# Gathering one tile at a time and evicting turned shares two PSUM banks at a time, in a dynamic-filter convolution followed by a bottleneck block

## The chip, the cores and the metric

The kernel runs on one core of a Trainium2 chip. The engines named below are PE (TensorE, matrix products and transposes), ACT (ScalarE), DVE (VectorE), POOL (GpSimd) and SP (SyncE, which issues most of the DMAs). PE writes into PSUM, eight banks of 512 fp32 columns on 128 partitions; the other engines copy from there into SBUF. Times are microseconds on the device, of one execution of the whole program. Where a time is read inside the program it counts from the start of the profiled span.

## The reference

Everything is fp32. The first layer takes x of 4 x 256 x 64 x 64 and computes, for every pixel, 49 weights from x itself; these then weigh 49 shifted copies of x:

```python
k = conv(x, w1, rhs_dilation=2, padding=6) + b1      # 7x7, 256 -> 128 channels
k = conv(k, w2) + b2                                 # 1x1, 128 -> 49
attn = softmax(k, axis=1)                            # over the 49 taps
y = einsum('bkchw,bkhw->bchw', shifts, attn)         # shifts[k] = x moved by 2*(u-3), 2*(v-3)
```

The second layer is a bottleneck block on y: 1x1 convolution (256 to 64), batch normalisation and ReLU, 3x3 convolution, batch normalisation and ReLU, 1x1 convolution (64 to 256), batch normalisation, plus y, ReLU. The normalisations use the moments of the data.

## The kernel before, in words

The two convolutions of the first layer are folded into one with 49 output channels, and this one is computed from sums of columns of x at several points, so that fewer products are needed. The input lies in one large SBUF buffer, the arena: four planes of 8192 columns each, xs[h][c]. Up to about 411 us PE runs the products of L361 over "pieces" of this buffer, while DVE makes their operands (L321 to L324 in make, L337 in add_columns) and combines the results (L371, L398, L389 on ACT). Final products (L437) turn the combined sums, called sides, into logits, and final_add puts them into place with DVE additions (L371).

The logits are handled in eight groups (s, h), s = 0 to 3 and h = 0 or 1. For each group five steps follow.

- exponents: DVE takes the maximum over the 49 taps (L479) and subtracts it (L480); ACT takes the exponential (L481).
- totals: DVE sums (L488) and takes the reciprocal (L489).
- shares: DVE multiplies and writes the four parts j = 0 to 3 into a row of zeroed, padded columns (L502). For the group (3,1), POOL clears a few places again (L513).
- turns: for each j, eight PE transposes (L522) fill two PSUM banks with the turned shares; two ACT copies (L529) bring them into the matrix amat, one for each half g of the columns. In the last group, (3,1), the copy of g = 1 is DVE's (L527).
- zero_edges: after both groups of an s, POOL clears ten strips of amat (L537).

amat takes the place of x in the arena, columns 0 to 32767, when the planes of x are no longer needed in that place. Its order is (g, x, c, m, e): g has a stride of 16384 columns, x (the group and j % 2) 1024, c (j // 2) 512. Some other things lie in the same columns while amat is being filled: planes of x that later pieces still read, the sides of the last chunk (from column 8192), and two of the padded rows (11264 to 15935 and 28096 to 32767).

All this is written in an order fixed by hand (manual_schedule, from L571). Inside the convolution, single steps are put between its groups of products by the table fill (L541 to L567): the turns (0,0) stand in one chunk, the turns (0,1) and (1,0) in a later one, and the first two turns of (1,1) in the last. After the convolution come the rest of the turns (1,1), the last final products, and then the sequence of L730 to L751. Engines other than the writer are released by semaphores, which the framework places from what each instruction reads and writes.

Then the gather computes y. A unit is one of the batch's images b and one quarter q of its pixels; 16 units are taken in the order of `units`. For a unit, more_xt loads the rows of x in pixel-major form by three DMAs (load_xt, L142, L143, L148), and shift_xt makes a second tile, shifted by 64 rows, with one ACT copy (L152, partitions 0 to 63) and two POOL copies (L153, L154). For each unit and each half of the channels, gather (L823) makes 32 products (64 records in the trace): for c = 0 from the tile itself and for c = 1 from the shifted one, 7 inner block pairs and one pair of edge blocks for each, by two halves of the output partitions. keep_y (L847) evicts the two banks, by DVE (L858) or, for the second half of the channels, by ACT (L856), and stores y by a DMA (L859). The convolution to 64 channels (conv1, L862) follows for every pair of units, and more_xt is called for the units that come. Two units' tiles exist at a time. From L777 a second part in hand-written order covers the first call of more_xt; the order of what follows it comes from the framework.

The last stages are the 3x3 convolution, the moments for the third normalisation, and the 1x1 convolution to 256 channels with the output.

Of the kernel before, what the change touches and what calls it, by code (L numbers as in the profile page):

```python
# [42 lines left out]
F32 = mybir.dt.float32  # L43
AF = mybir.ActivationFunctionType
ALU = mybir.AluOpType
AX = mybir.AxisListType
PSUM = bass.MemoryType.PSUM

P = 128
# [51 lines left out]
def conv_seq_kernel(ctx: ExitStack, tc: tile.TileContext, xp, xt, w1, b1, w2t, b2, m1t, g1, be1,  # L101
                    m2t, g2, be2, m3t, g3, be3, z, mask, pavg, out, ydram):
    nc = tc.nc

    def pool(stack, name, bufs, space=None, **kw):
        if space is not None:
            kw["space"] = space
        return stack.enter_context(tc.tile_pool(name=name, bufs=bufs, **kw))
# [14 lines left out]
    smp = pool(ctx, "smp", 3)  # L123
# [9 lines left out]
    amat = arena[:, :AT].rearrange("p (g x c m e) -> p g x c m e", g=2, x=R // 2, c=2, e=4)  # L133
    XT = NT * C
    xts = {}
# [203 lines left out]
    def bank(cn, k):  # L339
        return accall[:, (6 * cn + k) % 8]  # L340
# [130 lines left out]
    def columns(s, h):  # L471

        return logit[:, 2 * s + h].rearrange("p j (w k) -> p j w k", k=K)

    def exponents(s, h):

        e = columns(s, h)
        mx = smp.tile([P, 4, 4], F32, tag="mx", name="mx")
        nc.vector.tensor_reduce(mx, e, AX.X, ALU.max)  # L479
        nc.vector.tensor_tensor(e, e, mx.unsqueeze(3).to_broadcast([P, 4, 4, K]), ALU.subtract)  # L480
        nc.scalar.activation(e, e, AF.Exp)  # L481

# [2 lines left out]
    def totals(s, h):  # L485

        sm = smp.tile([P, 4, 4], F32, tag="sm", name="sm")
        nc.vector.tensor_reduce(sm, columns(s, h), AX.X, ALU.add)  # L488
        nc.vector.reciprocal(sm, sm)  # L489
        factors[s, h] = sm  # L490
# [3 lines left out]
    def shares(s, h):  # L494

        e = columns(s, h)
        sm = factors.pop((s, h))
        row = pads[ROWS[s, h]]
        for j in range(4):
            o = 32 + 32 * (j % 2)  # L500
            taps = row[j][:, :, o : o + 32 * K7].rearrange("p w (u x) -> p w u x", x=32)[:, :, :, :K7]
            nc.vector.tensor_tensor(  # L502
                taps,
                e[:, j].rearrange("p w (u v) -> p w u v", v=K7),
                sm[:, j].unsqueeze(2).unsqueeze(3).to_broadcast([P, 4, K7, K7]),
                ALU.mult,
            )

            for w in range(3):
                if s == 0 and h == 0:  # L510
                    nc.gpsimd.memset(taps[:, w, :, : 3 - w], 0.0)
                if s == NS - 1 and h == 1:
                    nc.gpsimd.memset(taps[:, 3 - w, :, 4 + w :], 0.0)  # L513

    def turn(s, h, j, b0, shared=False):

        row = pads[ROWS[s, h]]
        pt = accall[:, b0 : b0 + 2].rearrange("p a (m n) -> p (a m) n", n=P)
        for k in range(2):
            for w in range(4):  # L520
                o = 35 - (WS * s + 4 * h + w) + P * k
                nc.tensor.transpose(pt[:, 4 * k + w, :], row[j][:, w, o : o + P], ident)  # L522
        for g in range(2):
            dst = amat[:, g, 2 * (2 * s + h) + j % 2, j // 2].rearrange("p (n k) e -> p k n e", k=2)
            src = pt[:, :, 64 * g : 64 * g + 64].rearrange("p (k w) n -> p k n w", k=2)
            if shared and g:
                nc.vector.tensor_copy(dst, src)  # L527
            else:
                nc.scalar.copy(dst, src)  # L529

    def zero_edges(s):

        for g in range(2):
            for c, above, below in ((0, ((0, 96),), ((96, P),)), (1, ((0, 32),), ((32, 64), (64, P)))):
                for block, parts in ((0, above), (2 * NT - 1, below)):
                    for p0, p1 in parts:
                        nc.gpsimd.memset(amat[p0:p1, g, 4 * s : 4 * s + 4, c, block :: 2 * NT, :], 0.0)  # L537
# [8 lines left out]

    second, third, between, final = ("pair", 1, 1), ("pair", 2, 1), ("last", LAST, 1), ("pair", NP - 1, 1)
    put(second, 0, 5, lambda b0: exponents(0, 0))
    put(second, 1, 1, lambda b0: (totals(0, 0), shares(0, 0)))
    put(third, 1, 2, lambda b0: exponents(0, 1))  # L550
    put(third, 2, 0, lambda b0: totals(0, 1))
    put(third, 2, 3, lambda b0: exponents(1, 0))
    put(third, 3, 0, lambda b0: totals(1, 0))
    put(between, 0, 1, lambda b0: shares(0, 1))
    for j in range(4):
        put(second, 2, j, lambda b0, j=j: turn(0, 0, j, b0))
        put(between, 0 if j < 3 else 1, (j + 3) % 6, lambda b0, j=j: turn(0, 1, j, b0))
        put(between if j < 3 else final, 1 if j < 3 else 0, j + 3 if j < 3 else 2, lambda b0, j=j: turn(1, 0, j, b0))
# [12 lines left out]
    with tc.manual_schedule(engines=engines):  # L571
# [66 lines left out]
        for q, (cn, h, sub, step, count) in enumerate(pieces):  # L638
            kind, n, c = chunks[cn]
# [19 lines left out]
            elif waiting and step:  # L659
                total, slots = len(waiting), 6 * (count - 1 - step) + 2  # L660
                for i in range(total):
                    s = (2 * i + 1) * slots // (2 * total)
# [25 lines left out]
            if kind == "early":  # L688
# [6 lines left out]
                pt = bank(cn, 6)[:, :K]  # L695
# [3 lines left out]
            elif step == count - 1 or (chunks[cn][0] == "pair" and cn != end and step == 1):  # L699
                k = uses.index((cn, h)) + 2  # L700
# [24 lines left out]
        def turns(s, h, js, shared=False):  # L725
            for j in js:
                turn(s, h, j, (6 * end + 2 + 2 * n_turn[0]) % 8, shared)
                n_turn[0] += 1
# [7 lines left out]
        turns(2, 0, (0, 1))  # L736
        run_adds()
        nc.gpsimd.memset(pads_flat[3], 0.0)
        exponents(3, 0)
        turns(2, 0, (2, 3))  # L740
        totals(2, 1)
        shares(2, 1)
        exponents(3, 1)
        turns(2, 1, range(4))
        zero_edges(2)
        for h in range(2):
            totals(3, h)
            shares(3, h)
        turns(3, 0, range(4))
        turns(3, 1, range(4), True)  # L750
        zero_edges(3)  # L751
# [71 lines left out]
    def gather(n, half):  # L823

        b, q = units[n]
        m = (b // 2 * Q + q) * 2 * NT
        pts = [bank(0) for c in range(2)]
        for edge in (False, True):
            for c in range(2):
                x = xts[b, q, c]  # L830
                for i in (0,) if edge else range(1, NT):

                    o = 64 * (i - 1)
                    blocks = slice(m, m + 2 * NT, 2 * NT - 1) if edge else slice(m + 2 * i - 1, m + 2 * i + 1)
                    dst = pts[c].rearrange("p (m n) -> p m n", n=64)
                    for part in HALVES:
                        nc.tensor.matmul(  # L837
                            dst[part, :: NT - 1] if edge else pts[c][part, o : o + 128],
                            x[:, i, half * P + part.start : half * P + part.stop],
                            amat[:, b % 2, :, c, blocks, :].rearrange("p x m e -> p m x e"),  # L840
                            start=(i == 1),
                            stop=edge,
                            skip_group_check=True,
                        )
        return pts
# [43 lines left out]
    for n in range(len(units)):  # L889
        pts = gather(n, 0)  # L890
        if n and n % 2 == 0:
            conv1(*units[n - 2])
        if n == 9:
            clear_h1(1)
            nc.gpsimd.memset(w2blk, 0.0)
            for k, (j, a, o_a) in enumerate(TAPS3):
                d = TAP_ROW3[k]
                nc.sync.dma_start(
                    out=w2blk[a * MID : (a + 1) * MID, 3 * j : 3 * j + 3, o_a * MID : (o_a + 1) * MID],
                    in_=m2t[:, 3 * d : 3 * d + 3, :],  # L900
                )
        keep_y(n, 0, pts)
        keep_y(n, 1, gather(n, 1))
        if n + 2 < len(units):
            more_xt(n + 2)
# [197 lines left out]
    for n, (slot, i, q) in enumerate(blocks):  # L1103
# [3 lines left out]
        pt = pb_.tile([P, 512], F32, tag="pb", name="pturn2")  # L1107
# [23 lines left out]
    pt = pb_.tile([P, 512], F32, tag="pb", name="pprod")  # L1131
# [3 lines left out]
    for half in range(NH):  # L1135
        c = slice(half * P, (half + 1) * P)
# [9 lines left out]
    for k, (b, i, half) in enumerate(blocks):  # L1146
        o = ops[k % 4]

        n = 256 if k in (0, len(blocks) - 1) else 512
        for lo in range(0, 512, n):  # L1150
            for q in (0, 2, 1, 3):
# [5 lines left out]
                dst = o[:, rows].rearrange("p (r a) (w c) -> p a c r w", a=2, c=2)[:, q // 2, q % 2]  # L1157
# [92 lines left out]
```

## Time and profile before

| | |
|---|---|
| median of three runs | 748.4 us (746.14 to 748.69) |
| the profiled execution | 747.49 us, span 745.7 us, granted clock 0.972 |
| PE busy | 683.6 us, 92% of the span |
| DVE busy | 515.7 us, 69% |
| ACT busy | 241.4 us, 32% |
| POOL busy | 139.3 us, 19% |
| chain that ended last | PE 67%, DVE 18%, DMA 7%, ACT 3% |
| its largest lines | L361 30%, L837 11%, L437 7% |
| copies of the turned shares (L529, 60 on ACT) | 31.1 us busy, 0.619 each |
| gather products (L837, 2048 records) | 115.2 us busy |

The stages are, in the span's time: weights and sorting of x to 70 us, the large convolution to 411, the last products, softmax and turns to 454, gather and conv1 to 602, the 3x3 convolution to 665, moments to 698, output to 746. In the timelines below a line gives the start, the duration, the engine, the line of the program, the operation, what it writes and reads, how many instructions of the kind follow each other there, and in brackets the idle time before them with what ended it.

### The profile page before, as it was taken

To read this page: it belongs to the slowest core of one execution; us is meant where nothing else is said; L and a number is where in the kernel's file an instruction comes from. 1 tells how busy PE (TensorE), PEld (TensorE's weight loads), DVE (VectorE), ACT (ScalarE), POOL (GpSimd) and SP (SyncE) were. 2 spreads that over 40 slices of the span, in tenths; PEclk is the share of its full clock that TensorE was granted. 3 is DMA by queue.
4 is the path that set the end of the run, shared out by engine and by line. 5 is a ranking of instruction groups with operands and counts; after the bars stand their busy time and mean duration, and the time that the engine had idled before them with its cause. 6 is when DMAs were issued, how large, how long until landed. Compare 5 with 4: busy or idle time off the path is not lost.

```text
span 745.7 us, 18077 instructions
## 1 busy us (share of the span) xinstructions
PE 683.6 (92%) x7856; PEld 564.1 (76%) x7856; DVE 515.7 (69%) x750; ACT 241.4 (32%) x431; POOL 139.3 (19%) x224
## 2 busy tenths in 40 slices
PE   4979799999999998999999989999989979979995
PEld 3958789989989997888888879888767844438542
DVE  2875989998967999898945893222322228944896
ACT  2846500000000002100220265333433355345696
POOL 0545711111110411000122053222222200000000
PEclk9999999999999999999999999999999989998997
DMA  8998721010410211010220404766676678343498
GB/s 359 379 413 322 260 74 37 21 37 21 136 37 8 80 49 36 21 37 2 102 67 2 128 5 126 267 222 218 213 236 213 226 282 309 102 155 113 170 394 338
DMA packets 51105, 115.87 MB, mean 155 GB/s; under 512 B 5970, under 2 KB 31186, under 8 KB 46418
## 3 DMA queue, kind: packets, MB, share of 16 engines
q1 hardware_dynamic: 50592, 111.20, 42.5%
q10 hardware_dynamic: 434, 3.51, 1.1%
q8 instruction: 62, 1.02, 0.6%
q14 instruction: 17, 0.14, 0.1%
HBM read 74.12 MB, written 40.58 MB: 154 GB/s over the span
## 4 chain that ended last, share of the span: by engine, by line
PE 67%; DVE 18%; DMA 7%; ACT 3%; issue 2%; POOL 1%; SPq 0%; DVEq 0%; ACTq 0%; POOLq 0%
PE acc L361 30%; PE acc L837 11%; PE acc L437 7%; DVE arena L1153 5%; PE pconv L1044 4%; PE acc L870 4%; DVE arena L371 3%; PE pdirect L1032 3%; DMA arena<-in_xt_dram 3%; DMA arena<-in_xp_dram 3%; PE acc L215 3%; PE acc L522 2%; PE moments L1114 1%; PE pturn L1109 1%; DMA arena<-in_w_dram 1%
## 5 line engine op out<-in xcount | busy, mean ns | idle before, releaser
L361 PE MATMUL acc<-arena 128*64 128x196 f32 (+2 forms) x3840 | 308.7, 311 | 9.1 <-ACT bias L698 4.9
L361 PEld LDWEIGHTS acc<-arena 128*64 128x64 f32 x3840 | 278.2, 137 | 32.7 <-ACT bias L698 5.1
L837 PE MATMUL acc<-arena 128*64 128x128 f32 x2048 | 115.2, 273 | 11.0 <-issue 6.8
L837 PEld LDWEIGHTS acc<-arena 128*64 128x64 f32 x2048 | 112.8, 137 | 16.5 <-issue 13.7
L389 ACT COPY arena<-acc 128x980 f32<-128x980 f32 (+2 forms) x11 | 9.9, 903 | 199.4 <-PE acc L437 127.8
L337 DVE TENSOR_TENSOR arena<-arena 128x1024 f32<-128x1024 f32 x40 | 51.5, 1288 | 18.6 <-PE acc L361 18.6
L238 POOL TENSOR_TENSOR arena<-arena 128x294 f32<-128x294 f32 x19 | 19.2, 1009 | 230.4 <-DMA arena<-wts_dram 230.4
L878 DVE BATCH_NORM_STATS2 st<-acc 128x6 f32<-128x512 f32 x16 | 11.1, 694 | 70.2 <-PE acc L870 70.2
L215 PE MATMUL acc<-arena 128*64 128x196 f32 (+1 forms) x392 | 40.1, 364 | 15.4 <-DMA arena<-in_w_dram 10.4
L152 ACT COPY arena<-arena 64x2048 f32<-64x2048 f32 x15 | 28.5, 1899 | 78.0 <-DMA arena<-in_xt_dram 78.0
L215 PEld LDWEIGHTS acc<-arena 128*64 128x64 f32 x392 | 33.7, 147 | 21.4 <-issue 7.9
L266 POOL COPY arena<-arena 128x256 f32<-128x256 f32 x48 | 40.3, 884 | 39.6 <-DMA arena<-in_xp_dram 39.6
L371 DVE TENSOR_TENSOR arena<-acc,arena 128x392 f32<-128x392 f32 (+6 forms) x63 | 31.2, 513 | 23.2 <-PE acc L437 22.4
L437 PE MATMUL acc<-arena,late 128*64 128x392 f32 (+2 forms) x192 | 45.4, 417 | 0.0
L437 PE MATMUL acc<-arena 128*64 128x392 f32 (+2 forms) x224 | 45.0, 399 | 0.3 <-DVE arena L371 0.3
L858 DVE COPY arena<-acc 128x256 f32<-128x256 f32 x64 | 23.2, 416 | 30.6 <-PE acc L837 29.1
L1095 PE MATMUL pconv<-arena,late 64*128 64x512 f32 (+1 forms) x144 | 43.4, 594 | 0.6 <-DVE arena L1153 0.6
L1158 ACT ACTIVATE arena<-arena 128x512 f32<-128x512 f32 (+1 forms) x72 | 43.4, 705 | 1.3 <-DVE arena L934 1.1
L1153 DVE SCALAR_TENSOR_TENSOR arena<-pconv,arena 128x512 f32<-128x512 f32 (+1 forms) x72 | 43.3, 682 | 0.0
L529 ACT COPY arena<-acc 128x512 f32<-128x512 f32 x60 | 31.1, 619 | 36.0 <-PE acc L522 34.6
L153 POOL COPY arena<-arena 64x1792 f32<-64x1792 f32 x15 | 25.2, 1678 | 91.7 <-DMA arena<-in_xt_dram 81.4
L321 DVE SCALAR_TENSOR_TENSOR arena<-arena 128x1024 f32<-128x1024 f32 x32 | 41.2, 1287 | 0.0
(137 smaller groups left out, 860.3 us busy)
## 6 DMA issues: line engine op xcount, KB each, us to landing
arena<-in_xp_dram SPq DMA_DIRECT2D x16, 1216.0 KB, 8.6
y_dram<-arena SPq DMA_DIRECT2D x32, 512.0 KB, 4.1
arena<-y_dram SPq DMA_DIRECT2D x32, 512.0 KB, 7.6
arena<-in_xt_dram SPq DMA_DIRECT2D x17, 896.0 KB, 6.5
out_dram<-arena SPq DMA_DIRECT2D x14, 1024.0 KB, 3.9
arena<-in_w_dram SPq DMA_DIRECT2D x4, 1568.0 KB, 11.4
arena<-wts_dram SPq DMA_DIRECT2D x18, 343.0 KB, 3.1
wts_dram<-arena ACTq DMA_DIRECT2D x2, 1715.0 KB, 9.9
```

Of the source, the lines that this page charges most:

```text
L215: nc.tensor.matmul(pw[part, o : o + n], wv[:, K7 - 1 - u, part], powers[:, u, :n], start=(u == 0), stop=(u == K7 - 1), skip_group_check=True,)
L266: by[who](d[:, SLOT[n], :, :, PLACE[b], 2 * e : 2 * e + 2, t0 : t0 + 4], raw[:, 2 * n + e :: 8, PAD : PAD + W].rearrange("p r (g w c) -> p ...
L321: lambda: f(t[:, 0], x[:, SLOT[2]], p * p, x[:, SLOT[0]], ALU.mult, ALU.add),
L337: nc.vector.tensor_tensor(sums, v[:, :, :, 0], v[:, :, :, 1], ALU.add)
L361: nc.tensor.matmul(pt[part, (lo - base) * K : (hi + 1 - base) * K], x[:, part], w[:, (lo - a) * K : (hi + 1 - a) * K], start=(i == 0 and k ...
L371: nc.vector.tensor_tensor(out, in0, in1, op)
L437: nc.tensor.matmul(pt[half, o : o + z], m, ca, start=(i == 0 and single is None), stop=(i == len(group) - 1), skip_group_check=True,)
L529: nc.scalar.copy(dst, src)
L837: nc.tensor.matmul(dst[part, :: NT - 1] if edge else pts[c][part, o : o + 128], x[:, i, half * P + part.start : half * P + part.stop], ama ...
L1095: nc.tensor.matmul(pt[:, :n], w3m[part, half * P : (half + 1) * P], h2[part, slot, q, lo : lo + n], start=True, stop=True)
L1153: nc.vector.scalar_tensor_tensor(v, conv3(b, q, i, half, lo, n), sc3[:, half : half + 1], v, ALU.mult, ALU.add)
L1158: nc.scalar.activation(dst, v.rearrange("p (r w) -> p r w", w=R), AF.Relu, bias=sh3[:, half : half + 1])
```

## The change

There are three parts. In the turn, the two copies of 512 columns, one for each g, become one copy of 1024 that takes both banks at once and writes both halves of amat. In the last group ACT copies the even j whole and DVE the odd j whole, where each j had been divided between them by g. In the closing sequence, the totals and shares of (2,1) move ahead of the turns (2,0) j = 2 and 3; the exponents of (3,0) come after these; of the exponents (3,1), the maximum is taken before the turns (2,1), and the subtraction and the exponential stand after zero_edges(2) and the shares (3,0). In the gather, the loop over c becomes the outer one: all inner and edge products on the tile, then all on the shifted tile. The number of products, transposes, DMAs and fills stays as it is.

```diff
+    peaks = {}
+
+    def maxima(s, h):
+
+        mx = smp.tile([P, 4, 4], F32, tag="mx", name="mx")
+        nc.vector.tensor_reduce(mx, columns(s, h), AX.X, ALU.max)
+        peaks[s, h] = mx
+
     def exponents(s, h):
 
-        e = columns(s, h)
-        mx = smp.tile([P, 4, 4], F32, tag="mx", name="mx")
-        nc.vector.tensor_reduce(mx, e, AX.X, ALU.max)
+        if (s, h) not in peaks:
+            maxima(s, h)
+        e, mx = columns(s, h), peaks.pop((s, h))
         nc.vector.tensor_tensor(e, e, mx.unsqueeze(3).to_broadcast([P, 4, 4, K]), ALU.subtract)
         nc.scalar.activation(e, e, AF.Exp)
...
                 nc.tensor.transpose(pt[:, 4 * k + w, :], row[j][:, w, o : o + P], ident)
-        for g in range(2):
-            dst = amat[:, g, 2 * (2 * s + h) + j % 2, j // 2].rearrange("p (n k) e -> p k n e", k=2)
-            src = pt[:, :, 64 * g : 64 * g + 64].rearrange("p (k w) n -> p k n w", k=2)
-            if shared and g:
-                nc.vector.tensor_copy(dst, src)
-            else:
-                nc.scalar.copy(dst, src)
+        dst = amat[:, :, 2 * (2 * s + h) + j % 2, j // 2].rearrange("p g (n k) e -> p g k n e", k=2)
+        src = pt.rearrange("p (k w) (g n) -> p g k n w", k=2, g=2)
+        if shared and j % 2:
+            nc.vector.tensor_copy(dst, src)
+        else:
+            nc.scalar.copy(dst, src)
...
-        exponents(3, 0)
-        turns(2, 0, (2, 3))
         totals(2, 1)
         shares(2, 1)
-        exponents(3, 1)
+        turns(2, 0, (2, 3))
+        exponents(3, 0)
+        maxima(3, 1)
         turns(2, 1, range(4))
         zero_edges(2)
-        for h in range(2):
-            totals(3, h)
-            shares(3, h)
+        totals(3, 0)
+        shares(3, 0)
+        exponents(3, 1)
+        totals(3, 1)
+        shares(3, 1)
         turns(3, 0, range(4))
         turns(3, 1, range(4), True)
         zero_edges(3)
...
-        for edge in (False, True):
-            for c in range(2):
-                x = xts[b, q, c]
+        for c in range(2):
+            x = xts[b, q, c]
+            for edge in (False, True):
                 for i in (0,) if edge else range(1, NT):
```

## Prediction

> **What bounds the kernel now.** I read the busy time by stage first. Until 411 us the stage of the big convolution is TensorE's; between 411 and 454 the last products, the softmax and the turns alternate; from 454 to 602 the gather runs. The columns are the stretch, its length, the busy time of PE, PEld, DVE, ACT and POOL with their counts, the granted clock, the DMA share and GB/s.
>
> ```profile
> 290.00:411.00 121.00, 117.47 (x1385) 103.47 (x1383) 95.18 (x114) 17.05 (x29) 18.16 (x34) 0.99 0.13 41
> 411.00:454.00 43.00, 38.04 (x389) 33.24 (x385) 34.33 (x68) 22.98 (x42) 14.06 (x36) 0.96 0.28 81
> 454.00:602.00 148.00, 137.59 (x2160) 121.54 (x2161) 43.80 (x100) 54.19 (x96) 33.44 (x49) 1.00 0.66 216
> ```
>
> PE is busy for 97%, 88% and 93% of them: what delays PE delays the end, and what only relieves ACT (14% busy in the first) gives nothing. Next I read the timelines around the turns (start, duration, engine, line). Four lines show a turn in the conv stage:
>
> ```profile
> 297.20 1.07 ACT L529 COPY arena<-acc 128x512 f32<-128x512 f32 x2 [1.43 <-PE acc L522]
> 297.46 1.21 DVE L321 SCALAR_TENSOR_TENSOR arena<-arena 128x1024 f32<-128x1024 f32 x1
> 298.42 1.06 PE L522 MATMUL acc<-late,arena 128*128 128x128 f32 x8
> 298.60 1.21 DVE L322 SCALAR_TENSOR_TENSOR arena<-arena 128x1024 f32<-128x1024 f32 x1
> ```
>
> The copies run while DVE reads the planes of x with L321 and L322. The same holds later (DVE reading x or the sides at 362.29, 363.43 and from 425.96 on):
>
> ```profile
> 362.29 1.22 DVE L321 SCALAR_TENSOR_TENSOR arena<-arena 128x1024 f32<-128x1024 f32 x1
> 427.61 2.05 ACT L529 COPY arena<-acc 128x512 f32<-128x512 f32 x4 [1.24 <-PE acc L522]
> 429.10 1.09 PE L522 MATMUL acc<-late,arena 128*128 128x128 f32 x8 [0.58 <-DVE arena L371]
> 430.12 4.48 PE L437 MATMUL acc<-arena 128*64 128x196 f32 x32
> ```
>
> The end of the turns and the start of the gather:
>
> ```profile
> 443.17 0.86 ACT L481 ACTIVATE arena<-arena 128x784 f32<-128x784 f32 x1 [1.48 <-DVE arena L480]
> 443.93 10.09 ACT L529 COPY arena<-acc 128x512 f32<-128x512 f32 x20
> 454.07 6.17 PE L837 MATMUL acc<-arena 128*64 128x128 f32 x108 [0.68 <-ACT arena L529]
> ```
>
> Two things are to be seen. Twenty copies follow each other every 0.504 us, although one alone lasts 0.59 (a pair 1.07): the next starts before the last has ended. And the first product of the gather, which reads c = 0 alone (the turns j = 0 and 1), waits for the very last copy, which wrote c = 1 (j = 3). So the wait goes by the stretch of addresses from the first to the last element touched, not by the elements. One stall of the gather:
>
> ```profile
> 487.78 1.90 ACT L152 COPY arena<-arena 64x2048 f32<-64x2048 f32 x1 [6.63 <-DMA arena<-in_xt_dram]
> 489.78 2.19 PE L837 MATMUL acc<-arena 128*64 128x128 f32 x36 [1.17 <-issue]
> ```
>
> PE stands before the shifted tile (c = 1) until ACT has made it from rows that came by DMA.
>
> **Part 1: one copy for both halves g.** amat is the first 32768 columns of the arena, g has stride 16384, and one old copy lies inside its own g. The new copy's stretch reaches from its place in g = 0 to its place in g = 1, more than 16384 columns. In these lie the planes of x that DVE still reads (L321, L322), the sides of the last chunk (from 8192: L371, L398, L437), two of the padded rows that shares fills (L502), zero_edges' blocks, and every other turn's output. All of those now wait for the copy and the copy for them; each copy also waits for the end of the one before.
>
> Price of a copy of 1024: ACT's copies from PSUM last 0.487 (392 elements), 0.649 (588) and 0.977 (980, from two banks): 0.83 ns an element, so 1.02. Lowest 0.97, two of the shortest pitches; highest 1.24, two of 0.619. On DVE four of 512 take 2.48, so 1.2 for 1024. A handover from one engine to another is 0.04 (copies end at 454.03, PE starts at 454.07) to 0.10; I take 0.05. [...] The sum goes by the rows: two copies in a stream 1.01, one merged copy 1.02, nothing gained.
>
> What the waits cost, turn by turn, in the time of before:
> - (0,0), from 293.57. Copy j1 waits for L321 (ends 298.67): it ends at 299.70 instead of 298.27. The transposes j2 use PSUM that this copy reads from and wait: 299.8 instead of 298.42. L322 waits for the copy, copy j2 for L322 (about 300.95), so j3 starts at about 302.2 instead of 300.74: **+1.45** for PE. DVE has cover: its L337 at 304.65 had waited 2.33 for PE.
> - (0,1), from 359.72. Copy j0 waits for L321, which DVE's order puts at 362.29 to 363.51; it ends at 364.6, and the transposes j1 start at 364.65 instead of 362.22: **+2.45**. The turns (1,0) behind it meet DVE work already done: 0.
> - (1,1), from 424.11. Copy j0 waits for L371 (427.37) and ends at 428.4; transposes j1 to 429.5, copy j1 430.57; then L371, L371, L398, which took 2.27 (428.38 to 430.65) and now wait for that copy: 432.87. Copy j2 433.94, transposes j3 435.05, copy j3 436.1, and the final products L437, which read the sides inside the stretch, start at 436.15 instead of 430.12: **+6.0**.
>
> **Part 2: the new order at the end.** Counted from the transposes (2,0) at 434.53, so that the delays above are left out. Shares (2,1) come earlier, 438.15 to 439.33 (they were 440.06 to 441.24). But copy (2,0) j2 waits for them: 440.4, j3 441.46. The transposes (2,1) write PSUM that the preceding copies must free, so PE and ACT alternate, 1.09 + 1.02 + two handovers = 2.2 a turn: copies end at 443.65, 445.85, 448.05, 450.25. The exponents (3,1) stand behind these four on ACT: 450.3 to 451.15 instead of 443.17; sums and shares (0.96, 0.25, 1.18) follow to 453.7; the twelve L513 fills on POOL behind them (0.62) and the transposes (3,1) are done before their copy's turn comes. zero_edges(2) on POOL waits for the last of the four, and its last eight fills take 1.99: 452.3. The first copy (3,0) waits for them, since they lie in its stretch: four copies at 1.06 to 456.55. Then (3,1): j0 on ACT to 457.6, j1 on DVE waits for it, 458.85; ACT's order has the shift of unit 1's tile (L152, 1.90) before j2, to 459.5; j2 ends at 460.57. The gather's first half starts at 460.65 instead of 454.07: **+6.6**. Copy j3 on DVE (461.8) is hidden under that half's 32 products (1.75). The shift itself moves from 454.05 into this chain: 0.65 of those 6.6.
>
> **Part 3: the gather.** Same products, 54.7 ns a record. The shifted tile is wanted 4 records later, 0.22; evictions of c = 0 start about 0.6 earlier, x's tile is freed 28 records (1.53) earlier, and SP issues L143 before the y store. Eight stalls before c = 1 (470.98, 489.78, 508.45, 527.79, 545.74, 548.83, 568.10, 586.17) sum to 10.33. What ends them is the row read above: L148 issued at 482.08, landed about 487.7, L152 1.90, PE. Between 478.8 and 484.4 the DMA engines are full, so freeing a tile earlier brings it little. At best 0.8 a stall, 5.3 (one is 0.45 only); at worst nothing. I take the first stall, where the DMA is not yet full, and little else: **-1.2**. That is nearer the lower end since the wait ends with a transfer.
>
> Sum: 1.45 + 2.45 + 6.0 + 6.6 - 1.2 = +15.3. The profiled execution took 747.49 (span 745.7 and 1.8 around it), 0.9 under the median of 748.4: 747.5 + 15.3 = 762.8. Upper end: about 14 copies on the path at 1.24 (+3.1), handovers of 0.10 (+1.3), no gain in the gather (+1.2): +20.9. Lower end: the conv stage swallows its 3.9, the gather gains 5.3, copies cost 0.97: 15.3 - 3.9 - 4.1 - 0.7 = +6.6.
>
> **The rivals.**
> 1. Faster, 742 to 744. The waits fall into slack: PE has other products queued, ACT stands idle, and earlier shares (1.9) cancel the alternation, so that the gather starts no later than before and its stalls shrink by 5.3: 747.5 - 5.3 = 742.2. For it: ACT's low load before 411, the stalls' 10.33. Against it: transposes stand in PE's queue in order, so nothing behind them passes. It decides if the gather starts less than 5 us late.
> 2. Partly absorbed, +4 to +10, 751.5 to 757.5: the waits of the conv stage vanish under PE's own 3.5 of idle time, or the order's gain covers part of the end.
> 3. The merged copy is dearer (a source that strides over two banks), 1.24 and more: +18 to +21, about 768.
> 4. No change, 747.5: if the late start were regained because the gather waits for transfers anyway. Against it: only unit 1's tile is loaded before the gather; the later loads start from the gather's own releases, so they shift with it.
>
> **How the numbers follow.** 0.5% (3.7 us) is what a measurement tells from no change. Serial waits as summed 0.64; dearer copy 0.10; partly absorbed 0.14; faster 0.08; no change 0.04. Point 763.0. 754 to 770 takes in the first two and the upper half of the absorbed case, 0.81; the likeliest case alone spans 758 to 767. Faster 0.08, same 0.04, slower 0.88.
>
> **What would show it.** Right: 30 ACT copies of 1024 at about 1.0 us that no longer overlap; DVE L322 and PE transposes idle behind them; (1,1) stretched by 6; the gather starting 16.5 later, at about 470.6 in the span, with L152 just before the last ACT copy; its own length 146 to 147. Wrong: DVE and ACT rows still overlapping at the turns (0,0) to (1,1), or stalls before c = 1 summing to under 6. The prediction fails most if the copy is far from 1.02, since about 14 of them lie end to end.

## The result, and the profile after

The changed kernel takes 766.14 us (median of four runs, 765.12 to 770.75) against 747.27 before: the ratio is 1.0264, 95% interval 1.0217 to 1.031. It is slower by 18.9 us. The profiled execution has a span of 763.8, 18.1 more than before.

The points at which the two traces can be laid beside each other are these (start of the named instructions in the span; the last column is how much the distance grew since the row above):

| point | before | after | growth | forecast |
|---|---|---|---|---|
| transposes (0,0), j = 0 | 293.57 | 292.40 | -1.17 | 0 |
| transposes (0,1), j = 0 | 359.72 | 359.78 | +1.23 | +1.45 |
| transposes (1,1), j = 0 | 424.11 | 428.18 | +4.01 | +2.45 |
| last final products L437 | 430.12 | 441.47 | +7.28 | +6.0 |
| transposes (2,0), j = 0 | 434.53 | 447.09 | +1.21 | 0 |
| first product of the gather | 454.07 | 476.05 | +9.42 | +6.6 |
| last conv1 | 602.07 | 621.43 | -2.62 | -1.2 |
| end of the span | 745.7 | 763.8 | -1.26 | 0 |

First the copies. In the groups of ACT by shape the merged copy is one row (count, busy time, mean ns, idle time before it and what ended it):

```profile
L536 ACT COPY arena<-acc 128x1024 f32<-128x1024 f32 x30 | 30.4, 1012 | 58.5 <-PE acc L530 33.0 <-DVE arena L321 14.6 <-DVE arena L371 2.9
```

A copy of 1024 takes 1.012, so the busy time hardly moved (30.4 against 31.1), and the idle time in front grew from 36.0 to 58.5. L321 and L371 now stand among what ACT waits for. The timeline of the turns (0,0) shows it one by one:

```profile
297.27 1.01 ACT L536 COPY arena<-acc 128x1024 f32<-128x1024 f32 x1 [2.68 <-DVE arena L321]
298.31 1.23 DVE L322 SCALAR_TENSOR_TENSOR arena<-arena 128x1024 f32<-128x1024 f32 x1 [1.13 <-ACT arena L536]
298.43 1.06 PE L530 MATMUL acc<-late,arena 128*128 128x128 f32 x8 [1.28 <-ACT arena L536]
```

The copy waits for DVE's reading of x, DVE's next reading waits for the copy, and PE for the copy too. Before, all three ran beside each other. The PE timeline at the end of the convolution and in the closing sequence:

```profile
432.66 1.09 PE L530 MATMUL acc<-late,arena 128*128 128x128 f32 x8 [2.15 <-ACT arena L536]
434.91 1.97 PE L530 MATMUL acc<-late,arena 128*128 128x128 f32 x8 [1.16 <-ACT arena L536]
438.35 1.97 PE L530 MATMUL acc<-late,arena 128*128 128x128 f32 x8 [1.47 <-ACT arena L536]
441.47 5.69 PE L437 MATMUL acc<-arena 128*64 128x196 f32 x32 [1.16 <-ACT arena L536]
...
453.94 1.26 PE L530 MATMUL acc<-late,arena 128*128 128x128 f32 x8 [3.14 <-ACT arena L536]
456.36 1.97 PE L530 MATMUL acc<-late,arena 128*128 128x128 f32 x8 [1.16 <-ACT arena L536]
459.48 1.97 PE L530 MATMUL acc<-late,arena 128*128 128x128 f32 x8 [1.16 <-ACT arena L536]
```

Each wait is for ACT's copy, as forecast. But the eight transposes of a turn last 1.97 where they took 1.09, and L437 takes 5.69 instead of 4.48. The windows over these stretches show what goes with it (the window and its length, PE busy with count, granted clock, DMA share, GB/s):

```profile
428.00:432.00 4.00, 2.33 (x24) 1.00 0.89 279
434.00:436.00 2.00, 1.09 (x5) 0.56 0.07 8
436.00:440.00 4.00, 2.53 (x13) 0.50 0.08 1
456.00:460.00 4.00, 2.48 (x11) 0.50 0.00 0
```

PE was granted 0.50 of its clock while it alternated with ACT. The gather's start, where ACT's and PE's timelines meet:

```profile
467.75 5.20 ACT L536 COPY arena<-acc 128x1024 f32<-128x1024 f32 x5 [1.31 <-POOL arena L544]
473.19 1.90 ACT L152 COPY arena<-arena 64x2048 f32<-64x2048 f32 x1 [0.25 <-DMA arena<-in_xt_dram]
475.00 1.00 ACT L536 COPY arena<-acc 128x1024 f32<-128x1024 f32 x1
476.05 4.15 PE L846 MATMUL acc<-arena 128*64 128x128 f32 x72 [2.56 <-ACT arena L536]
```

Five copies at 1.04 apiece, after waiting for POOL's zero_edges; then the shift, then the last copy on ACT. And a stall of the gather, the one that stood at 489.78:

```profile
511.63 1.97 PE L846 MATMUL acc<-arena 128*64 128x128 f32 x32 [0.88 <-issue]
```

The eight stalls that the prediction summed now come to 7.70, against 10.33.

### The profile page after: what moved, and what is told of

Read it like the earlier page. It is cut to its first block, busy times and chain, and to the rows that moved or that the text cites. A ratio compares the mean times of both kernels' runs of the same rounds, so it can differ in the third digit from the quotient of the medians.

```text
span 763.8 us, 18054 instructions
## 1 busy us (share of the span) xinstructions
PE 692.8 (91%) x7856; PEld 569.9 (75%) x7856; DVE 515.1 (67%) x748; ACT 241.3 (32%) x401; POOL 138.2 (18%) x224
## 4 chain that ended last, share of the span: by engine, by line
PE 68%; DVE 17%; ACT 5%; DMA 5%; issue 2%; POOL 1%; SPq 0%; ACTq 0%; DVEq 0%; POOLq 0%
PE acc L361 29%; PE acc L846 13%; PE acc L437 7%; DVE arena L1162 4%; PE pconv L1053 4%; PE acc L879 4%; PE pdirect L1041 3%; PE acc L530 3%; DVE arena L371 3%; DMA arena<-in_xp_dram 2%; DMA arena<-in_xt_dram 2%; PE acc L215 2%; ACT arena L536 2%; PE moments L1123 1%; PE pturn L1118 1%
## 5 line engine op out<-in xcount | busy, mean ns | idle before, releaser
L361 PE MATMUL acc<-arena 128*64 128x196 f32 (+2 forms) x3840 | 310.6, 313 | 8.3 <-ACT bias L705 4.1
L361 PEld LDWEIGHTS acc<-arena 128*64 128x64 f32 x3840 | 278.8, 138 | 33.0 <-ACT bias L705 4.4
L238 POOL TENSOR_TENSOR arena<-arena 128x294 f32<-128x294 f32 x19 | 21.4, 1128 | 233.9 <-DMA arena<-wts_dram 223.8
L530 PE MATMUL acc<-late,arena 128*128 128x128 f32 x256 | 39.4, 314 | 16.3 <-ACT arena L536 15.1
L371 DVE TENSOR_TENSOR arena<-acc,arena 128x392 f32<-128x392 f32 (+6 forms) x63 | 31.4, 514 | 31.3 <-PE acc L437 28.4
L530 PEld LDWEIGHTS acc<-late,arena 128*128 128x128 f32 x256 | 33.7, 163 | 22.5 <-ACT arena L536 17.1
L536 ACT COPY arena<-acc 128x1024 f32<-128x1024 f32 x30 | 30.4, 1012 | 58.5 <-PE acc L530 33.0
L437 PE MATMUL acc<-arena 128*64 128x392 f32 (+2 forms) x224 | 46.2, 415 | 1.5 <-ACT arena L536 1.2
L437 PE MATMUL acc<-arena,late 128*64 128x392 f32 (+2 forms) x192 | 45.4, 417 | 0.0
L266 POOL COPY arena<-arena 128x256 f32<-128x256 f32 x48 | 38.4, 841 | 37.6 <-DMA arena<-in_xp_dram 37.6
L152 ACT COPY arena<-arena 64x2048 f32<-64x2048 f32 x15 | 28.5, 1899 | 50.8 <-DMA arena<-in_xt_dram 49.2
```

The source lines that it names most:

```text
L361: nc.tensor.matmul(pt[part, (lo - base) * K : (hi + 1 - base) * K], x[:, part], w[:, (lo - a) * K : (hi + 1 - a) * K], start=(i == 0 and k ...
L371: nc.vector.tensor_tensor(out, in0, in1, op)
L437: nc.tensor.matmul(pt[half, o : o + z], m, ca, start=(i == 0 and single is None), stop=(i == len(group) - 1), skip_group_check=True,)
```

## Experiments

The kernel before was measured anew with every group of runs, so the time that a run is set against differs a little from one to the next (744.13 to 745.17).

### One part at a time

In split_copies the changed kernel has the old turn again:

```diff
-        dst = amat[:, :, 2 * (2 * s + h) + j % 2, j // 2].rearrange("p g (n k) e -> p g k n e", k=2)
-        src = pt.rearrange("p (k w) (g n) -> p g k n w", k=2, g=2)
-        if shared and j % 2:
-            nc.vector.tensor_copy(dst, src)
-        else:
-            nc.scalar.copy(dst, src)
+        for g in range(2):
+            dst = amat[:, g, 2 * (2 * s + h) + j % 2, j // 2].rearrange("p (n k) e -> p k n e", k=2)
+            src = pt[:, :, 64 * g : 64 * g + 64].rearrange("p (k w) n -> p k n w", k=2)
+            if shared and g:
+                nc.vector.tensor_copy(dst, src)
+            else:
+                nc.scalar.copy(dst, src)
```

> The changed kernel with the old turn: two copies of 512, one for each g; new order and new gather kept. Theory A (the merged copy's wide stretch of addresses makes the waits, the other two parts are harmless): the serial waits go, the shares (2,1) come 1.9 us earlier and the gather keeps its 2.6, so 747.3 - 1.9 - 2.6 = 743, 741 to 745. Theory B (the new order is what delays the turns): still slower than before, 752 or more.

Measured: 744.71 against 745.13 before, ratio 0.998 (0.9956 to 1.0004). The whole loss is gone, so Theory B falls. A's number was 743 and its range reached to 745; the gain of 4.5 that it counted did not come. The turns and the gather's start, ACT and then PE:

```profile
434.18 4.01 ACT L537 COPY arena<-acc 128x512 f32<-128x512 f32 x8 [0.41 <-PE acc L530]
```

```profile
442.43 3.69 PE L530 MATMUL acc<-late,arena 128*128 128x128 f32 x32 [1.67 <-DVE arena L510]
447.00 3.85 PE L530 MATMUL acc<-late,arena 128*128 128x128 f32 x32 [0.89 <-DVE arena L510]
451.54 1.97 PE L847 MATMUL acc<-arena 128*64 128x128 f32 x32 [0.69 <-DVE arena L535]
```

Copies stream again at half a microsecond each. The earlier shares (2,1) save less than 1.9, since PE now waits twice for the shares of (3,0) and (3,1), 1.67 and 0.89.

In merge_alone the kernel before has only the merged copy, the same edit the other way round.

> The kernel before with only the copy merged over both halves g. Theory A (wide stretch): the conv stage and the turns (1,1) lose what the changed kernel lost there, about 13.5 us, and the closing turns some 8 to 10 more: 768 to 772, above the changed kernel. Theory B (the merged copy hurts only together with the new order): 755 or less.

Measured: 771.29 against 745.13, ratio 1.0336 (1.0302 to 1.037). A holds: the merged copy alone costs 26 us, more than the whole change. From the transposes (1,1) j = 0 to the gather 50.35 pass (425.80 to 476.15), in the changed kernel 47.87. So together with merged copies the new order takes back 2.5. From there to the last conv1 the old loops take 150.3 (476.15 to 626.41), the new ones 145.4; but 3.6 of these 4.9 are PE's busy time (141.3 against 137.7), as its clock was granted at 0.51 to 0.64 from 476 to 480 and from 514 to 518, where the changed kernel's gather has it at 1.00. So this isn't the price of the loops alone.

In gather_alone the kernel before has only the loops of the gather exchanged (the last hunk of the change).

> The kernel before with only the gather's loops exchanged. Theory A (the gather's own part of the change gains what the two traces show between the start of the gather and the end of conv1, 2.6 us): 744.7, 744 to 746, and the stalls before c = 1 sum to about 7 to 8 instead of 10.3. Theory B (the gather only gained because it started 20 us late, with more of its first tiles at hand): 747 to 748, stalls still at 10.

Measured: 742.95 against 745.13, ratio 0.9972 (0.9944 to 1.0). The stalls sum to 7.45, inside A's 7 to 8, and the median fell by 2.2; but the interval ends at 1.0, so the time doesn't prove a gain. Nor do the stalls: order_alone, the next run, has the old loops and no late start, and its stalls sum to 7.02. From the first product to the last conv1 this run takes 147.43, before 148.00 and order_alone 148.22. What the new loops are worth by themselves stays open.

In order_alone the kernel before has only the new closing sequence (the hunks in exponents and from L736 on), with the old copies and the old gather.

> The kernel before with only the closing sequence reordered and the last group's copies divided as before. Theory A (the order is worth what the run with split copies showed against the one with the gather alone): the gather starts 1.0 earlier against the start of the turns (2,0), and the time lies between 0 and 2 below before. Theory B (the order alone is worth the 1.9 by which shares (2,1) come earlier): 2 or more below before.

Measured: 743.61 against 744.13, ratio 0.9993 (0.9973 to 1.0013): no difference that can be told. In the trace the gather starts 18.47 after the first transposes (2,0) instead of 19.54 before, the 1.0 of A; B falls.

### Is it the stretch or the size of the copy?

In copy_per_bank each turn of the changed kernel is evicted by two copies of 512, as before, but cut by PSUM bank and not by g:

```diff
-        dst = amat[:, :, 2 * (2 * s + h) + j % 2, j // 2].rearrange("p g (n k) e -> p g k n e", k=2)
-        src = pt.rearrange("p (k w) (g n) -> p g k n w", k=2, g=2)
-        if shared and j % 2:
-            nc.vector.tensor_copy(dst, src)
-        else:
-            nc.scalar.copy(dst, src)
+        for k in range(2):
+            dst = amat[:, :, 2 * (2 * s + h) + j % 2, j // 2].rearrange("p g (n k) e -> p g k n e", k=2)[:, :, k]
+            src = pt[:, 4 * k : 4 * k + 4, :].rearrange("p w (g n) -> p g n w", g=2)
+            if shared and j % 2:
+                nc.vector.tensor_copy(dst, src)
+            else:
+                nc.scalar.copy(dst, src)
```

> The changed kernel with each copy cut in two by PSUM bank: 512 elements each as before the change, as many copies as before the change, each from one bank, but each writes both halves g, so its stretch of addresses stays wide. Theory A (the stretch costs): about 766 plus 0.1 to 0.2 for each of some 14 turns on the path, 766 to 770. Theory B (a copy of 1024 from two banks is what costs): back to the old copies' time, 743 to 748.

Measured: 777.87 against 745.13, ratio 1.0428 (1.0393 to 1.0462). The size is excluded: copies just as small and as many as before the change, but with the wide stretch, cost 33 us. A's own number, 766 to 770, was too low by 8 or more. The ACT groups of split_copies and of copy_per_bank, in this order:

```profile
L537 ACT COPY arena<-acc 128x512 f32<-128x512 f32 x60 | 31.3, 621 | 34.6 <-PE acc L530 33.4 <-issue 1.2
```

```profile
L537 ACT COPY arena<-acc 128x512 f32<-128x512 f32 x60 | 35.1, 585 | 61.6 <-PE acc L530 28.4 <-DVE arena L321 16.0 <-DVE arena L322 6.5
```

A single copy is even a little shorter (585 against 621), but two in a row take 1.20 and not 1.07, and behind the longer waits PE's clock is low in one more place: the first products of the gather come after a wait of 5.25 and run at 0.50, where the changed kernel has them at 1.00 after 2.56.

```profile
484.04 16.19 PE L847 MATMUL acc<-arena 128*64 128x128 f32 x256 [5.25 <-ACT arena L537]
```

```profile
484.00:488.00 4.00, 3.96 (x38) 0.50 0.00 0
```

Of the 14.1 that its span has over the changed kernel's, 8.0 lie before the gather (484.04 against 476.05), the rest in it and behind it. How it divides between copies and clock there was not separated.

### Is it PE's clock?

In kept_busy the changed kernel gets work for PE that nothing reads: transposes of the identity into the banks that the turn then overwrites, so that PE has something to do while the copies run.

```diff
+    warm = {(1, 1, 2): 8, (1, 1, 3): 8, (2, 1, 0): 16, (2, 1, 1): 7, (2, 1, 2): 7, (2, 1, 3): 7}
+
+    def keep_busy(pt, n):
+        for i in range(n):
+            nc.tensor.transpose(pt[:, i % 8, :], ident, ident)
+
     def turn(s, h, j, b0, shared=False):
...
         pt = accall[:, b0 : b0 + 2].rearrange("p a (m n) -> p (a m) n", n=P)
+        keep_busy(pt, warm.get((s, h, j), 0))
         for k in range(2):
```

> The changed kernel with extra work for PE: transposes of the identity, overwritten afterwards, ahead of the real transposes of the turns (1,1) j = 2, 3 (8 each) and (2,1) j = 0 (16) and j = 1, 2, 3 (7 each). They go into the banks that the turn itself then fills. Theory A (PE's granted clock falls to 0.5 because PE stands, which doubles transposes and products behind the waits): transposes of (1,1) and (2,1) last 1.09 again instead of 1.97, the products L437 4.5 instead of 5.7, so the gather starts 4 to 6 us earlier and the time is 4 to 6 below the changed kernel's. Theory B (the transposes are slow for another reason, such as copies reading PSUM at the same time): 1.97 stays, and the extra work gains nothing or costs 1 to 3. The extra transposes also tell what a turn of (2,1) waits for: if for its PSUM banks, as the prediction has it, they wait for the copy before as well; if only for the padded row that it reads, they run at once.

Measured: 759.64 against 744.13, ratio 1.0211 (1.0167 to 1.0256), where the change has 1.0264. Its span is 4.5 shorter than the changed kernel's, and the gather starts at 471.35 instead of 476.05, 4.70 earlier, with the transposes (1,1) j = 0 at the same place (428.19 and 428.18). The intervals of the two ratios overlap, so the verdict rests on the trace. PE's timeline and the clock:

```profile
453.17 0.93 PE L527 MATMUL acc<-late 128*128 128x128 f32 x7
454.49 1.09 PE L537 MATMUL acc<-late,arena 128*128 128x128 f32 x8 [0.39 <-ACT arena L543]
455.42 0.93 PE L527 MATMUL acc<-late 128*128 128x128 f32 x7
456.74 1.09 PE L537 MATMUL acc<-late,arena 128*128 128x128 f32 x8 [0.39 <-ACT arena L543]
```

```profile
456.00:460.00 4.00, 3.21 (x28) 1.00 0.00 0
```

With 53 more transposes the turns (2,1) are faster: 1.09 each at clock 1.00, one turn every 2.25 and no longer every 3.13, and L437 takes 4.24. That is Theory A, though not everywhere: at (1,1) the stand of 2.16 ahead of j = 1, where no work was added, still brought the clock to 0.50 (434 to 436), and the transposes j = 1 and 2 took 1.57 and 1.43; and the first products of the gather, after a stand of 2.78, ran at 0.50 until 474. The lines show a second thing. The extra transposes (L527) write the very banks that the next turn uses and run at once; only the real ones wait for ACT. So that wait of the turns (2,1) is not for PSUM. What the real ones have beside the bank is the padded row, at columns 11264 to 15935, which lies inside the stretch of the copy before.

### What a stall of the gather is made of

The stalls that remained ended, nearly all, with L152, which makes partitions 0 to 63 of the shifted tile in one copy and so waits for all three DMAs of the tile. In split_shift it is cut, on top of split_copies:

```diff
-        nc.scalar.copy(t[:MID], x[MID:])
+        nc.scalar.copy(t[:MID, 1:], x[MID:, 1:])
+        nc.scalar.copy(t[:MID, 0], x[MID:, 0])
```

> The changed kernel with the old copies, and with the ACT copy of the shifted tile (L152) cut in two: blocks 1 to 7 (1792 columns, which need the DMA L143 alone) and block 0 (256 columns, which needs L142 and L148). In the gather's new loop order the shifted tile's block 0 is wanted last. Theory A (the stalls before c = 1 are the last transfer plus a copy of 1.90 behind it): the stalls of 4.7 to 7.7 shrink to below 3, and the time is 2 to 5 below the run with old copies alone, 740 to 743 against a before of 745. Theory B (the DMA engines as such are late): the stalls only move, within 1 us of the run with old copies alone.

Measured: 733.91 against 744.13, ratio 0.9861 (0.9829 to 0.9894). The stalls sum to 1.17, less than A's 3, and the gain is larger than its 5. ACT's timeline and PE's over the same time:

```profile
480.80 1.69 ACT L152 COPY arena<-arena 64x1792 f32<-64x1792 f32 x1 [2.00 <-DMA arena<-in_xt_dram]
...
484.73 0.40 ACT L153 COPY arena<-arena 64x256 f32<-64x256 f32 x1 [1.19 <-DMA arena<-in_xt_dram]
```

```profile
473.90 14.14 PE L848 MATMUL acc<-arena 128*64 128x128 f32 x256
487.88 3.60 PE L881 MATMUL acc<-arena,late 128*64 128x512 f32 x16
491.31 14.14 PE L848 MATMUL acc<-arena 128*64 128x128 f32 x256
```

Blocks 1 to 7 are copied at 480.80, and block 0 only at 484.73, after 1.19 of waiting for its own DMA; PE goes through without a pause. The one stall that is left, 1.17 at 539.47, is of another kind: PE waits there for the DMA of the tile itself.

Two more runs tell how much of this needs the rest. In shift_alone the kernel before has only this cut; in gather_shift it has the cut and the new loops.

> The kernel before, its gather loops and copies unchanged, with only the ACT copy of the shifted tile cut in two (blocks 1 to 7, block 0). Theory A (the wait of the shifted tile for the last transfer is the whole stall, the loop order hardly matters): the edges are last in the old order too, so the stalls go as they did with the new order, from 10.3 to about 2, and the time is 7 to 9 below before. Theory B (the cut pays only with the new order, which frees and wants the tiles differently): 2 to 5 below before, with stalls of 5 or more left.

> The kernel before with the gather's new loop order and the cut copy of the shifted tile; closing sequence and copies of the turns as before. Theory A (the new closing order is worth 0 to 1): 9 to 10 below before, as split_shift. Theory B (the closing order is what made split_shift that fast): 7 or less below before.

Measured: shift_alone 737.49 against 745.17, ratio 0.9901 (0.9867 to 0.9935), with one stall of 1.85 left (again for the tile's own DMA); gather_shift 736.24 against 745.17, ratio 0.9879 (0.9844 to 0.9914), with 0.18 left. The cut alone gives 7.7 of the 10.2; Theory A of both runs holds, with gather_shift's 8.9 just under its 9 to 10. The intervals of the three runs overlap, so what order and loops add to the cut isn't settled. All three beat both kernels.

## Why the prediction was right, and where its terms were off

The direction and the main mechanism are shown: split_copies takes the loss away, merge_alone brings it back without the other parts, and copy_per_bank brings it back with copies of the old size. The price of a copy (1.02 forecast, 1.014 by its own 0.83 ns an element, 1.012 measured), 1.2 on DVE (1.225), the waits at L321, L398 and L437, POOL's zero_edges before the copies (3,0), and the shift before the last copy on ACT all stand in the trace as they were worked out. So rival 1 (waits in slack), rival 2 (partly absorbed) and rival 3 (a dearer copy) fall; rival 4 too, as the gather took back only 2.6 of 22.

What was off, step by step:

- (0,0): +1.23 for +1.45. Right; inside the turns, from j = 0 to j = 3, it is 8.38 against 7.17, +1.21. The longer way to (0,1) takes 66.15 or 67.75 to 67.84 in the kernels with the old copies, for a reason given at the end of this list that neither before nor after has.
- (0,1): +4.01 for +2.45. The wait itself is there: j = 1 starts 2.47 later (364.75 against 362.22, of which 0.06 came from before). What the sum lacks came after it: products L361 took 2.72 instead of 1.55, the transposes behind them 1.55 instead of 1.10, together 1.6.
- (1,1): +7.28 for +6.0, and +1.21 in L437, which the sum had as unchanged. Transposes j = 3 took 0.88 more, L437 1.21 more; the slow transposes j = 2 are hidden, as their copy waits for L398 anyway.
- The closing sequence: +9.42 for +6.6. Four turns of (2,1) took 0.17, 0.88, 0.88 and 0.88 more for their transposes, 2.8.
- The gather: -2.62 for -1.2. I had taken nearly the lower end, on the ground that the DMA engines are full (busy share 1.00 from 478.8 to 484.4 in the trace of before). The stalls shrank by 2.6; gather_alone has 7.45 without the late start, but order_alone has 7.02 with the old loops, so it isn't shown that the new loops did it. Two readings were off: of the eight stalls, the one at 545.74 stands before the tile itself and not before c = 1, and the 1.75 of the first half are 32 records, that is 16 products. The row that I quoted held the better reading of the stalls: what waits is a copy for the last of three transfers, and split_shift shows that PE needs that last piece much later.
- The end: -1.26 where nothing was forecast, and -1.17 before the first turn. No instruction of the change lies there; the seven kernels whose instructions are the same up to the transposes (2,0) reach these between 432.57 (shift_alone) and 437.15 (gather_shift), so traces differ by up to 4.6 for no cause that was changed. One such difference can be seen: between (0,0) and (0,1) PE stands for 1.85 to 1.87 before the products L436 (at 322 to 326). In five of the seven the clock then falls to 0.50 for three to four microseconds, and these five are the ones that take 1.6 to 1.7 more on that way; in before and order_alone it stays at 1.00. What makes up the rest no run here settles.

The clock's additions sum to 1.6 + 0.9 + 1.2 + 2.8 = 6.5, which is the excess before the gather (23.2 measured between the first turn and the gather, 16.5 forecast). The step that was mis-sized is therefore the pricing of the waits: they were worked out with PE's durations at full clock, 1.09 a turn, throughout. Kept_busy shows 4.7 of it to be the clock; the 1.6 at (0,1) and a part at (1,1) were not given extra work there, and for them only the granted clock in the windows speaks. That the point, 763.0, came within 3.1 of the measured 766.1 is partly luck: the 6.7 that were missing before the gather were offset by 1.4 more in the gather and by 2.4 that nothing in the change explains. The profile of before could have warned. Its window after the one stand of 2.32 in the closing sequence:

```profile
440.00:444.00 4.00, 3.43 (x21) 0.69 0.00 0
```

The other step that was wrong is a reason, not a number: that the transposes (2,1) wait since they "write PSUM that the preceding copies must free". Before the change the same turns used the same banks without such a wait, and in kept_busy writes into them did not wait. What is left is the padded row, which the copy's stretch covers without writing it. (The turns that stand together in one chunk of the convolution share one pair of banks, so there the reason can hold.) And the new order was counted as bringing shares (2,1) forward by 1.9; alone it is worth 1.0 at the gather's start and nothing that the time shows.

## What to carry to other kernels

Before merging two instructions that write far apart, look at what lies between the two places: where dependencies are tracked from the first to the last address, the merged instruction waits for all of it and all of it waits for the instruction, and a saving of nothing turned into 19 to 26 us here. Price a wait of PE at the clock that PE may be granted afterwards, 0.50 in the worst case here, and read the clock in short windows after every stand of the profile that one has. And where a copy stands between transfers and PE, ask which of the pieces PE needs first: cutting one copy along its transfers was worth 7.7 us, more than any part of this change gained.

## What the runs showed of the hardware

In the changed kernel PE's granted clock fell to 0.50 after stands of no more than 3.14. At (0,1) it was a single stand of 2.40: the transposes began at 364.75 at full clock, and from 366 to 369 the clock was 0.50.

```profile
364.75 1.10 PE L530 MATMUL acc<-late,arena 128*128 128x128 f32 x8 [2.40 <-ACT arena L536]
365.77 2.72 PE L361 MATMUL acc<-arena 128*64 128x196 f32 x16
```

```profile
366.00:368.00 2.00, 2.00 (x16) 0.50 0.03 8
```

At (1,1) the clock was still 1.00 after a stand of 2.15 and fell within the next, of 1.16, 1.09 of work later (0.71 from 433.80 to 434.90, then 0.50); at (2,1) it fell after one of 3.14 (0.87 from 454 to 455, then 0.50). Further stands of 1.16 to 1.47, with 1.97 of work between, then went with 0.50 for as long as they lasted (436 to 444 and 456 to 464). With stands of 0.39 (kept_busy) it stayed at 1.00 (454 to 462), and so it did around a stand of 1.16 ahead of L437 there (440 to 444).

The length of a stand alone did not decide it here. Before the gather, the clock was 1.00 after 2.56 in the changed kernel, and 0.50 after 2.78 in kept_busy. Clearest is the stand of 1.85 to 1.87 before L436, the same in every kernel: in five of the eleven traces the clock fell to 0.50 behind it, and in six it stayed at 1.00. Here is the clock soon after it, first before (stand until 325.32), then in split_copies (until 322.17):

```profile
326.00:328.00 2.00, 2.00 (x36) 1.00 0.00 0
```

```profile
323.00:325.00 2.00, 2.00 (x24) 0.55 0.00 0
```

The sum above, an estimate from the durations in the changed kernel's trace, puts the clock's part at 6.5 us. What decides whether the clock falls behind a stand, no run here shows.
